# Rope's tables from TensorE, bias and norm rows spread by TensorE, and cosine products in place in PSUM

## The chip, the cores and the metric

The kernel runs on one core of a Trainium2 chip. Its time is the time on the device in microseconds (us), from the start of the program to its end. Engines are named as the profile names them: PE is TensorE (PEld its weight loads), DVE is VectorE, ACT is ScalarE, POOL is GpSimd, SP is the engine that here only issues DMAs. An entry such as SPq or ACTq is the sequencer of an engine, which issues DMAs.

## What is computed

A block of linear attention and a gated feed-forward layer (RWKV's channel mixing), each followed by a layer norm over the sum with its input. The input has 16 sequences of 1024 tokens with 512 channels in fp32. Only the attention half is touched by the change:

```python
qkv = x @ Wqkv.T + bqkv
q, k, v = split(qkv)
q = q * rsqrt(mean(q*q) + eps) * gq      # rmsnorm, the same for k with gk
k = k * rsqrt(mean(k*k) + eps) * gk
# rope, per head of 32 channels, position l: pairs (r, i)
out_r = r*cos[l] - i*sin[l];  out_i = r*sin[l] + i*cos[l]
qf, kf = relu(q), relu(k)
# per sequence and head: sum over l of [v, 1] x kf, applied to qf, divided by the last row
```

The launch puts the channels of q and k in an order in which each head has its 16 real parts first and then its 16 imaginary parts.

## The kernel before

**Tiles.** Work goes by tiles of 128 tokens: 128 tiles, 8 to a sequence (a block). Each tile of x is loaded twice, turned (`xt`, channels on partitions) for the projections and straight (`xn`) for the sum over tokens. Every fp32 operand of a product is split into two halves, `h` (a cast to fp32r) by ScalarE and `l` (the remainder) by VectorE, and a product is three passes (h by h, h by l, l by h). A projection of one tile to q or to k is therefore 4 chunks of channels by 3 passes, 12 products of 512 columns into one PSUM bank (`proj`, L415 to L429).

**One slot a tile.** `slot(i)` (L579) is called for i from 0 to 127. In it: the projections q(i) and k(i); the halves of the next tile's `xt` (`split_x`, L284) and of this tile's `xn`; `add_kx(i - 1)` (L465), 12 products that add k times x of the tile before into four banks `kx0` to `kx3` of a pool of their own; `rope(i)`; then `tables(i + 1)` and `seed(i + 1)`. Ends of blocks add `finish_a` to `finish_c`. From the sixth slot on one further weight chunk is loaded and split a slot (`late_weight`). The feed-forward half follows from 1200 us on; a few of its tiles are drawn into the slots.

**Seeds and banks.** Products that are not on the `kx` banks take banks from a ring of four (`mm`, `bank`, L97). Before a projection ScalarE copies the bias row, which lies spread over all partitions in `b_qk`, into its bank (`seed`, L318, by `seeded`, L136), and the products add to it. A bank can be seeded again once rope has read it for the last time.

**Rope.** `rope` (L433) reads q, then k, from PSUM: ScalarE takes the sum of squares (L438); VectorE multiplies by the sine table into `t2` (L441), by the cosine table into `ro` (L442), and adds the two with halves of heads swapped (L443). q goes to DRAM as `q_d`; k is scaled and cut at zero by ScalarE (L451), cast to `kh` (L454), and VectorE makes `kl` (L455). POOL makes the reciprocal root (L121) and the running sum of k over a block (L460, L462).

**Tables.** The tables hold the norm weight times cosine or sine for the 128 positions of a tile, one each for q and k: four of 128 by 512 (`tables`, L330). Since a sequence has 8 tiles, they are computed for tiles 0 to 7 and stored to DRAM (`tab_d`, L349); later tiles load them (L340). Each has a single buffer. POOL computes them with two forms of multiply (L345 for cosine, L348 for sine), from the norm weights spread over partitions (`g_qk`) and from `cos` and `sn`.

**The start (L352 to L386).** Eight products on zeros; the load of the first `xt`; `b_qk` and `g_qk` as loads that spread a row over 128 partitions (512 KB each); the eight weight chunks of q and k (n = 0 to 3 for q, 4 to 7 for k), loaded in turn by SP's and ScalarE's queues, each split by `split_w` (L310).

**Order.** The lists of each engine are not the order of the source: a planner simulates the program with its own costs and lays out each engine's instructions, taking what is ready and giving what comes first in the source the first claim. On the chip every engine then works through its list in order.

Of the kernel before, what the change touches and what calls it, by code (L numbers as in the profile page):

```python
# [8 lines left out]
F32 = mybir.dt.float32  # L9
# [25 lines left out]
def kernel(  # L35
# [41 lines left out]
    def f32(ap):  # L77
        return ap.bitcast(F32)
# [186 lines left out]
    with ExitStack() as a_ctx:  # L265
# [56 lines left out]
        def rows(tl):  # L322
            return tl.rearrange("p (h i) -> p h i", i=HH)

        def halves(tl):
            return tl.rearrange("p (h two i) -> p h two i", two=2, i=HH)
# [3 lines left out]
        def tables(i):  # L330

            t = i % 8
            if i < 8:
                tab_d[t] = dram.tile([P, 2, 2, DIM], F32, name=f"tab_d{t}")
            for j in range(2):
                for n in (1, 0):
                    tb = wa.tile([P, DIM], F32, tag=f"tab{j}{n}", name=f"tab{j}{n}{i}")
                    tab[i, j, n] = tb
                    if i >= 8:
                        nc.sync.dma_start(out=tb, in_=tab_d[t][:, j, n, :])  # L340
                        continue
                    g = g_qk[:, j * DIM : (j + 1) * DIM]
                    if n == 0:
                        c = cos[:, t, :].unsqueeze(1).to_broadcast([P, 2 * HEADS, HH])
                        G.tensor_mul(rows(tb), rows(g), c)  # L345
                    else:
                        c = sn[:, t, :, :].unsqueeze(1).to_broadcast([P, HEADS, 2, HH])
                        G.tensor_mul(halves(tb), halves(g), c)  # L348
                    nc.sync.dma_start(out=tab_d[t][:, j, n, :], in_=tb)  # L349


        m0 = te.tile([P, 2, DIM], F32R, tag="m", bufs=2, name="m0")  # L352
        V.memset(f32(m0[:, 0, :]), 0.0)
        for n in range(8):
            T.matmul(bank(f"pswarm{n}"), lhsT=m0[:, 0, 0:P], rhs=m0[:, 0, :], start=True, stop=True)
        load_xt(0)
        b_qk = ca.tile([P, 2 * DIM], F32, name="b_qk")
        nc.scalar.dma_start(out=b_qk, in_=bqkv[0 : 2 * DIM].partition_broadcast(P))
        split_x(0)
        g_qk = wp.tile([P, 2 * DIM], F32, tag="m", bufs=NC_, name="g_qk")  # L360
        cos = ca.tile([P, 8, HH], F32, name="cos")
        sin = tp.tile([P, 8, HH], F32, tag="y", bufs=2, name="sin")

        sn = ca.tile([P, 8, 2, HH], F32, name="sn")
        for j in range(2):
            cols = slice(j * DIM, (j + 1) * DIM)
            for c in range(NC_):
                n = NC_ * j + c
                split_w(
                    w_qk["h"][:, c, cols],  # L370
                    w_qk["l"][:, c, cols],
                    wqkv[:, c, cols],
                    V,
                    (nc.sync, nc.scalar)[c % 2],
                    *(("x", XA), ("q", 3))[n >= XA],
                )
            if j == 0:
                seed(0)
                nc.scalar.dma_start(out=g_qk, in_=gqk.partition_broadcast(P))
                nc.sync.dma_start(out=cos, in_=cos_t)  # L380
                nc.sync.dma_start(out=sin, in_=sin_t)
                G.tensor_copy(sn[:, :, 0, :], sin)
                G.tensor_scalar(sn[:, :, 1, :], sin, -1.0, None, ALU.mult)
                tables(0)
        load_xt(1)
        load_xn(0)  # L386
        mu, omm = {}, {}

        def constants():
# [43 lines left out]
        def rope(i, ps):  # L433
# [3 lines left out]
            for j in range(2):  # L437
                S.activation(junk(f"{i}{j}"), ps[j], AF.Square, accum_out=ss[:, j : j + 1])  # L438
                r = wa.tile([P, DIM], F32, tag=f"ro{j}", bufs=1 + j, name=f"ro{j}{i}")
                t2 = wa.tile([P, DIM], F32, tag="t2", name=f"t2{j}{i}")  # L440
                V.tensor_mul(t2, ps[j], tab.pop((i, j, 1)))  # L441
                V.tensor_mul(r, ps[j], tab.pop((i, j, 0)))  # L442
                V.tensor_add(halves(r), halves(r), halves(t2)[:, :, ::-1, :])  # L443
                ro.append(r)
                if j == 0:
                    q_d[i] = dram.tile([P, DIM], F32, name=f"q_d{i}")
                    nc.sync.dma_start(out=q_d[i], in_=r)
            V.tensor_scalar(ss, ss, 1.0 / DIM, RMS_EPS, ALU.mult, ALU.add)  # L448
            rsqrt(rstd_all[:, i, :], ss)
            k = ro[1]  # L450
            S.activation(k, k, AF.Relu, scale=rstd_all[:, i, 1:2])  # L451
            kh = tk.tile([P, DIM], F32R, tag="kh", bufs=2, name=f"kh{i}")
            kl = tk.tile([P, DIM], F32R, tag="kl", bufs=2, name=f"kl{i}")
            S.copy(kh, k)  # L454
            V.tensor_sub(kl, k, f32(kh))  # L455
            b, t = divmod(i, 8)
            ros[i] = k
# [111 lines left out]
        def late_weight():  # L569
# [6 lines left out]
            split_w(m[:, 0, :], m[:, 1, :], w[:, c, :], V, nc.sync)  # L576
            nc.sync.dma_start(out=w_d[n][:, c, :, :], in_=f32(m))

        def slot(i):  # L579
            last = i == N - 1  # L580
            if i + 2 < N:
# [1 line left out]
            b, t = divmod(i - 2, 8)  # L583
            if b >= 0 and t == 7:
                finish_a(b)
            qk = [proj(i, 0), proj(i, 1)]
            if not last:
                split_x(i + 1)
            split_xn(i)
            if not last:  # L590
# [9 lines left out]
            state[i] = rope(i, qk)  # L600
            if not last:
                tables(i + 1)
                seed(i + 1)
            if i == 2:
                with tc.issue_after(load.ins):
                    constants()
# [277 lines left out]
```

## Time and profile before

| what | value |
|---|---|
| median of 3 runs | 2749.24 us (2747.41 to 2749.43) |
| profiled execution, own time | 2751.16 us |
| profiled execution, span of the core | 2749.4 us |
| granted TensorE clock, mean | 0.996 |
| products (and transposes) issued | 12520 |
| PE busy, 0 to 8 us | 3.80 us |
| PE busy, 20 to 28 us | 8.00 us |
| PE busy, 1300 to 2749 us | 1441.93 of 1449 us |
| DMA, 0 to 8 and 8 to 20 us | 237 and 268 GB/s |

The profile is of one execution. Its span runs from the first to the last instruction of the core; the own time of that execution is 1.8 us more. PE's busy time counts overlapping products once, so that it says little about how close they follow each other; the number of products in a stretch, times the spacing of two that follow directly, says more. A group's line gives source line, engine, operation, output and inputs, shape and count, then busy time and the mean duration of one in ns, then how long the engine had stood idle before them and for whom. A line on waits names the waiting engine and line, whom it waited for, and the total, the number and the longest of the waits.

### The profile page before, as it was taken

What the parts mean: (1) busy time and instruction counts of PE and PEld (TensorE: products, weight loads), DVE (VectorE), ACT (ScalarE), POOL (GpSimd) and SP (SyncE); (2) the same over time, 40 slices, a digit from 0 to 9 for tenths busy, and PEclk for the clock granted to TensorE, in tenths of its full rate; (3) what the DMA queues carried; (4) which work ended last, traced back from release to release, by engine and by line L of the source; (5) the groups of instructions that cost most, each with busy time, mean ns of one, the idle gap of its engine ahead of it and who ended that gap; (6) DMA issues with size and microseconds to landing.
All of it is one profiled execution on the core that took longest, in us unless ns stands there. A gap on an engine that the chain in (4) does not pass through costs nothing.

```text
span 2749.4 us, 40113 instructions
## 1 busy us (share of the span) xinstructions
PE 2698.3 (98%) x12520; PEld 2227.0 (81%) x12520; DVE 2197.8 (80%) x4874; ACT 1878.3 (68%) x3807; POOL 724.5 (26%) x804
## 2 busy tenths in 40 slices
PE   8899999999999999998999999999999999999998
PEld 6687888888888788876888888888888888888887
DVE  8888887788888788878787878788787878787874
ACT  4566655666655556557777777777777777777775
POOL 6421222222222222223222222222222222222221
PEclk9999999999999999999999999999999999999999
DMA  6698778777777777764323231322223232313210
GB/s 216 217 308 292 235 234 265 226 229 222 222 227 230 228 236 241 236 216 163 102 65 108 93 115 55 114 89 91 86 92 108 66 108 92 116 54 116 69 58 31
DMA packets 230854, 431.17 MB, mean 157 GB/s; under 512 B 24544, under 2 KB 24800, under 8 KB 230640
## 3 DMA queue, kind: packets, MB, share of 16 engines
q1 hardware_dynamic: 229776, 426.51, 48.6%
q10 hardware_dynamic: 864, 2.10, 0.2%
q8 instruction: 99, 1.62, 0.2%
q14 instruction: 115, 0.94, 0.1%
HBM read 313.14 MB, written 115.38 MB: 156 GB/s over the span
## 4 chain that ended last, share of the span: by engine, by line
PE 66%; DVE 11%; issue 5%; DMA 5%; ACT 4%; POOL 1%; SPq 0%; DVEq 0%; ACTq 0%; POOLq 0%
PE psk L157 13%; PE psr L157 12%; PE psv L157 12%; PE psy L157 12%; PE pskx L477 4%; PE psq L421 4%; PE psk L421 3%; DVE ro L442 3%; DVE t L441 2%; PE pst L142 2%; PE psqt L142 2%; DMA q_d<-ro 2%; DVE ro L443 2%; DMA q<-q_d 1%; DVE kl L455 1%
## 5 line engine op out<-in xcount | busy, mean ns | idle before, releaser
L157 PE MATMUL psk<-mkh,w_k 128*128 128x512 f32 x1024 | 336.8, 396 | 0.0
L157 PE MATMUL psv<-w_v,kah 128*128 128x512 f32 x1024 | 321.8, 395 | 2.3 <-DVE qtl L213 1.2
L157 PE MATMUL psr<-w_r,mrh 128*128 128x512 f32 x1024 | 322.7, 396 | 1.1 <-ACT r L693 1.1
L157 PE MATMUL psy<-mb,qth 128*128 128x512 f32 x1024 | 316.7, 391 | 3.1 <-ACT qth L212 3.1
L121 POOL TENSOR_TENSOR rstd_all<-ss,mhalf 128x2 f32<-128x2 f32 x128 | 111.1, 868 | 682.7 <-DVE ss L448 651.9
L157 PEld LDWEIGHTS psy<-mb,qth 128*128 128x128 f32 x1024 | 192.5, 188 | 43.4 <-ACT qth L212 3.6
L249 DVE TENSOR_TENSOR y<-psy,g_out 128x512 f32<-128x512 f32 x128 | 88.3, 690 | 171.9 <-PE psy L157 171.6
L157 PEld LDWEIGHTS psk<-mkh,w_k 128*128 128x128 f32 x1024 | 192.3, 188 | 39.1
L157 PEld LDWEIGHTS psv<-w_v,kah 128*128 128x128 f32 x1024 | 187.6, 188 | 39.2 <-DVE qtl L213 1.6
L157 PEld LDWEIGHTS psr<-w_r,mrh 128*128 128x128 f32 x1024 | 187.5, 188 | 38.2 <-ACT r L693 1.5
L668 POOL TENSOR_TENSOR mkl<-mixk,mkh 128x512 fp32r<-128x512 f32 x128 | 175.6, 1372 | 144.0 <-ACT mkh L667 144.0
L421 PE MATMUL psq<-wqk_h,xh 128*128 128x512 f32 x512 | 202.3, 395 | 5.3 <-ACT wqk_h L313 2.7
L421 PE MATMUL psk<-wqk_h,xh 128*128 128x512 f32 x512 | 200.4, 391 | 1.4 <-ACT wqk_h L313 1.3
L421 PE MATMUL psk<-wqk_l,xh 128*128 128x512 f32 x512 | 200.1, 391 | 1.3 <-DVE wqk_l L314 1.3
L157 PE MATMUL psr<-w_r,mrl 128*128 128x512 f32 x512 | 200.7, 392 | 0.0
L157 PE MATMUL psy<-mb,qtl 128*128 128x512 f32 x512 | 200.4, 391 | 0.2 <-DVE qtl L213 0.2
L421 PE MATMUL psq<-wqk_h,xl 128*128 128x512 f32 x512 | 200.5, 392 | 0.0
L421 PE MATMUL psq<-wqk_l,xh 128*128 128x512 f32 x512 | 200.2, 391 | 0.2 <-DVE wqk_l L314 0.2
L157 PE MATMUL psv<-w_v,kal 128*128 128x512 f32 x512 | 200.1, 391 | 0.0
L421 PE MATMUL psk<-wqk_h,xl 128*128 128x512 f32 x512 | 199.8, 390 | 0.0
L157 PE MATMUL psk<-mkl,w_k 128*128 128x512 f32 x512 | 199.7, 390 | 0.0
L136 ACT COPY psk<-b_qk 128x512 f32<-128x512 f32 x128 | 75.8, 593 | 161.2 <-DVE ro L442 159.0
(147 smaller groups left out, 7219.1 us busy)
## 6 DMA issues: line engine op xcount, KB each, us to landing
tab<-tab_d SPq DMA_DIRECT2D x480, 256.0 KB
xt<-in_xt_dram SPq DMA_DIRECT2D x128, 256.0 KB
xn<-in_x_dram SPq DMA_DIRECT2D x128, 256.0 KB
q_d<-ro SPq DMA_DIRECT2D x128, 256.0 KB
m_d<-m SPq DMA_DIRECT2D x64, 512.0 KB
mb<-m_d SPq DMA_DIRECT2D x64, 512.0 KB
q<-q_d SPq DMA_DIRECT2D x128, 256.0 KB
x<-in_x_dram SPq DMA_DIRECT2D x128, 256.0 KB
```

What stands on the lines that cost most here:

```text
L121: G.tensor_tensor(dst, src, mhalf[:, 0 : src.shape[1]], ALU.pow)
L136: S.copy(ps, src)
L142: T.matmul(ps[:, n * P : (n + 1) * P], lhsT=b, rhs=ident, is_transpose=True, start=(n == 0), stop=(n == NC_ - 1), skip_group_check=True,)
L157: T.matmul(ps, lhsT=a[u][:, rows], rhs=b[w][:, cols], start=(afresh and c == 0 and k == 0), stop=(c == n - 1 and k == 2), skip_group_check ...
L249: V.tensor_mul(y, ps, g_out)
L421: T.matmul(ps, lhsT=a[i][:, c, :], rhs=w_qk[b][:, c, cols], start=False, stop=(c == NC_ - 1 and n == 2), skip_group_check=True,)
L441: V.tensor_mul(t2, ps[j], tab.pop((i, j, 1)))
L442: V.tensor_mul(r, ps[j], tab.pop((i, j, 0)))
L443: V.tensor_add(halves(r), halves(r), halves(t2)[:, :, ::-1, :])
L455: V.tensor_sub(kl, k, f32(kh))
L477: T.matmul(ps_kx[b][c], lhsT=a[:, c * P : (c + 1) * P], rhs=r, start=(t == 0 and n == 0), stop=(t == 7 and n == 2),)
L668: (V if n == "r" and s != 1 else G).tensor_sub(ml, m, f32(mh))
```

## The change

- `tables` for tiles 0 to 7: each table is one product on TensorE with 96 rows, `cs` (cosine and sine of the tile's positions, turned, in a high half twice and a low half) by `gt` (a mask that picks the angle's row, times the norm weight, in high and low halves). ScalarE copies the result to the table's buffer. Tiles 0 and 1 use the `kx` banks, the others the ring of four.
- The rows of bias and of norm weight are loaded as four rows of 2 KB into partitions 0, 32, 64 and 96 of a zeroed tile, split into halves, and spread over the partitions by products with 0/1 matrices (`sel_b`, `sel_g`). The bias goes straight into the banks of the first tile's q and k and is copied from there to `b_qk`.
- Five products on zeros in place of eight. The weights of q are split first, then the angles and norm weights are prepared, then the weights of k, with the load of the second `xt` behind the first of these. The second tile's seed and projection q(1) come ahead of k(0).
- `rope`: the cosine product is written in place in its PSUM bank, and the add reads it from there. `kh` is made by an activation of its own from k, ahead of the one that scales and cuts k.

```diff
@@ tables(i) @@
-                    g = g_qk[:, j * DIM : (j + 1) * DIM]
-                    if n == 0:
-                        c = cos[:, t, :].unsqueeze(1).to_broadcast([P, 2 * HEADS, HH])
-                        G.tensor_mul(rows(tb), rows(g), c)
-                    else:
-                        c = sn[:, t, :, :].unsqueeze(1).to_broadcast([P, HEADS, 2, HH])
-                        G.tensor_mul(halves(tb), halves(g), c)
+                    ps = kx_bank(2 * j + n) if i < 2 else bank(f"pstab{i}{j}{n}")
+                    T.matmul(ps, lhsT=cs[0:KT, t, :], rhs=gt[j][0:KT, n, :], start=True, stop=True)
+                    S.copy(tb, ps)
                     nc.sync.dma_start(out=tab_d[t][:, j, n, :], in_=tb)
+        def kx_bank(c):
+            return pa.tile([P, DIM], F32, tag=f"kx{c}", bufs=1, name=f"psb{c}")
@@ the start @@
-        for n in range(8):
+        for n in range(5):
             T.matmul(bank(f"pswarm{n}"), lhsT=m0[:, 0, 0:P], rhs=m0[:, 0, :], start=True, stop=True)
+        row = tp.tile([P, DIM], F32, tag="q", bufs=3, name="row")
+        V.memset(row, 0.0)
         load_xt(0)
+        for n, (src, j) in enumerate(((bqkv, 0), (bqkv, 1), (gqk, 0), (gqk, 1))):
+            nc.scalar.dma_start(
+                out=row[n * DH : n * DH + 1, :],
+                in_=src[j * DIM : (j + 1) * DIM].unsqueeze(0),
+            )
+        angle = [tp.tile([P, 8, HH], F32, tag="y", bufs=2, name=f"angle{n}") for n in range(2)]
+        for n, src in enumerate((cos_t, sin_t)):
+            nc.scalar.dma_start(out=angle[n], in_=src)
...
+        S.copy(row_h, row)
+        V.tensor_sub(row_l, row, f32(row_h))
         b_qk = ca.tile([P, 2 * DIM], F32, name="b_qk")
-        nc.scalar.dma_start(out=b_qk, in_=bqkv[0 : 2 * DIM].partition_broadcast(P))
+        for j in range(2):
+            first[0, j] = bank(f"ps{'qk'[j]}0")
+            for n, r in enumerate((row_h, row_l)):
+                T.matmul(first[0, j], lhsT=sel_b[:, j, :], rhs=r, start=(n == 0), stop=(n == 1))
+            S.copy(b_qk[:, j * DIM : (j + 1) * DIM], first[0, j])
         split_x(0)
...
+        for c in range(NC_):
+            split_qk(0, c)
+        cs3 = wp.tile([P, 8, P], F32, tag="m", bufs=NC_, name="cs3")[:, :, 0:KT]
+        for n in range(2):
+            G.tensor_copy(
+                cs3.rearrange("p t (r n i) -> p t r n i", r=3, n=2)[:, :, :, n, :],
+                angle[n].unsqueeze(2).to_broadcast([P, 8, 3, HH]),
+            )
...
+            for t in range(NC_):
+                T.matmul(ps[0:KT, t * P : (t + 1) * P], lhsT=cs3[:, NC_ * n + t, :], rhs=ident, is_transpose=True, ...)
+            S.copy(cs[0:KT, part, :], groups(ps)[0:KT])
+            low = slice(2 * DH, KT)
+            V.tensor_sub(cs[low, part, :], groups(ps)[low], f32(cs[low, part, :]))
...
+            for n, r in enumerate((row_h, row_l)):
+                T.matmul(ps, lhsT=sel_g[:, j, n, :], rhs=r, start=(n == 0), stop=(n == 1))
+            V.tensor_mul(halves(gt[j][:, 1, :]), halves(ps), msk[:, 1:3, :]...)
+            V.tensor_mul(rows(gt[j][:, 0, :]), rows(ps), msk[:, 0, :]...)
+        split_qk(1, 0)
         load_xt(1)
+        for c in range(1, NC_):
+            split_qk(1, c)
         load_xn(0)
+        seed(1)
+        tables(0)
@@ rope(i, ps) @@
-                V.tensor_mul(r, ps[j], tab.pop((i, j, 0)))
-                V.tensor_add(halves(r), halves(r), halves(t2)[:, :, ::-1, :])
+                V.tensor_mul(ps[j], ps[j], tab.pop((i, j, 0)))
+                V.tensor_add(halves(r), halves(ps[j]), halves(t2)[:, :, ::-1, :])
...
-            S.activation(k, k, AF.Relu, scale=rstd_all[:, i, 1:2])
-            S.copy(kh, k)
+            S.activation(kh, k, AF.Relu, scale=rstd_all[:, i, 1:2])
+            S.activation(k, k, AF.Relu, scale=rstd_all[:, i, 1:2])
@@ slot(i) @@
-            qk = [proj(i, 0), proj(i, 1)]
-            if not last:
+            if i == 0:
+                qk = [proj(0, 0)]
+                split_x(1)
+                ahead.append(proj(1, 0))
+                qk.append(proj(0, 1))
+            else:
+                qk = [ahead.pop() if ahead else proj(i, 0), proj(i, 1)]
+            if 0 < i < N - 1:
                 split_x(i + 1)
```

## The prediction

> **What bounds the kernel now.** I read the page's first part, then busy time by stretches, then TensorE's waits in the stretch that loses most, then the groups of that stretch. The page:
>
> ```profile
> PE 2698.3 (98%) x12520; PEld 2227.0 (81%) x12520; DVE 2197.8 (80%) x4874; ACT 1878.3 (68%) x3807; POOL 724.5 (26%) x804
> ```
>
> TensorE sets the time. At full clock a 512-column product follows the one before after 0.227 us (starts 22.29, 22.52, 22.74 in the timeline), so a product added costs 0.227 us and the only other thing to win is time in which none is issued. Where that lies (stretch: length, busy time and count of each engine):
>
> ```profile
> core 0: us, PE busy (x) PEld busy (x) DVE busy (x) ACT busy (x) POOL busy (x), PEclk, DMA share, GB/s
> 8.00:20.00 12.00, 9.23 (x24) 6.46 (x25) 8.95 (x9) 6.69 (x13) 7.20 (x6) 0.72 0.76 268
> 28.00:125.00 97.00, 83.85 (x349) 63.78 (x348) 84.79 (x112) 50.94 (x107) 57.66 (x42) 0.98 0.63 211
> 125.00:300.00 175.00, 173.06 (x792) 141.74 (x792) 146.06 (x252) 108.63 (x229) 38.20 (x36) 1.00 0.85 281
> 300.00:1200.00 900.00, 892.18 (x4103) 741.42 (x4102) 728.35 (x1271) 536.38 (x1143) 202.56 (x190) 1.00 0.74 233
> 1200.00:1300.00 100.00, 86.23 (x406) 68.42 (x405) 78.16 (x174) 65.81 (x131) 34.63 (x35) 0.98 0.53 179
> ```
>
> From 28 to 125 us there are 349 products: 333 of 512 columns, 8 of 256 and 8 of 128, at 0.227, 0.171 and 0.108 us: 77.8 us of work in 97, so 19.2 us are lost. In 300 to 1200 the same count of start-to-start excess gives 4.6 us. Who is waited for, 28 to 125 (total, times, longest):
>
> ```profile
> PE pskx L477 <- ACT kh L454: 8.7, 8, 2.4
> PE pskx L477 <- DVE kl L455: 3.3, 4, 1.0
> PE pskv L520 <- DVE ro L442: 0.7, 1, 0.7
> PE psq L421 <- ACT psq L136: 0.3, 1, 0.3
> ```
>
> These are 13.0 us; the rest is the slow restart after each wait and half clock at 50 to 53 us. kh and kl come late because rope does. The groups of 28 to 125, and the add again in 300 to 1200 (last line):
>
> ```profile
> L345 POOL TENSOR_TENSOR tab<-g_qk,cos 128x512 f32<-128x512 f32 x13 | 22.0, 1691 | 0.0
> L348 POOL TENSOR_TENSOR tab<-g_qk,sn 128x512 f32<-128x512 f32 x12 | 16.8, 1403 | 9.4 <-DVE t L441 9.3
> L443 DVE TENSOR_TENSOR ro<-ro,t 128x512 f32<-128x512 f32 x20 | 19.4, 972 | 0.2
> L442 DVE TENSOR_TENSOR ro<-psq,tab 128x512 f32<-128x512 f32 x10 | 6.8, 681 | 1.3 <-DMA q_d<-ro 1.3
> ...
> L443 DVE TENSOR_TENSOR ro<-ro,t 128x512 f32<-128x512 f32 x194 | 133.2, 687 | 2.7
> ```
>
> While POOL multiplies tables, VectorE's operations with both inputs in SBUF grow (the add 972 against 687 ns, xnl 1286 against 895, kl 1192 against 772); those with one input in PSUM do not (681).
>
> **Part 1, tables on TensorE.** POOL loses 38.8 us in that stretch. VectorE gets back 20 x 0.285 + 10 x 0.39 + 10 x 0.42 + 9 x 0.44 (L448, 599 against 158 ns) = 17.8 us, and stands at 67 us instead of 85. ScalarE gets four copies a tile at 0.59 us (its copies and squares read or write PSUM in 0.59): 28 of them for tiles 1 to 7, 16.5 us, on top of 50.9: 76% of some 89 us. TensorE gets 28 products, +6.4 us, on the path. The 19.2 us: at 300 to 1200 the loss is under 0.1 us a tile with VectorE at 81%, but here ScalarE is fuller, four PSUM banks serve six tiles a turn (q, k, four tables), and a table's copy must wait until rope has read the table before it (one buffer each), with the seeds queued behind it on ScalarE. Chain from the end of q: square 0.78, t2 0.69, copy 0.59, seed 0.59, some 0.5 of handovers: 3.2 us, against k (2.7) and kx (2.7) as cover. Bounds 1 and 12 us of loss; I take 0.5 us a tile, 4.0: **-15.2 and +6.4**.
>
> **Part 2, the start.** Two 512 KB broadcasts go; 5.1 MB land in the first 20 us, 255 GB/s, so k's weights, whose casts waited until 13.0 and 14.9 us, can land 3 to 4 us sooner. Against it: row loads wait for a memset and their six small issues (four rows, two angles, 0.35 us each) stand on ScalarE's queue with two of q's four weights. A landing also holds up unrelated issues:
>
> ```profile
> SPq L381 <- DMA b_qk<-in_bqkv_dram: 3.0, 1, 3.0
> ```
>
> The load of sin waited for the bias to land; more transfers ahead of the weights make more such turns, the small ones short. First product of q before: 7.98 us. After: rows landed about 5.2 (issue at 2 to 3; xt took 4.9 us beside a broadcast, so 4.5 to 7.9 are the ends, and 2 KB rows are taken near the lower), row_h 0.62, row_l 0.69, two products 0.5, copy of the bank to b_qk 0.59 before q may accumulate in it, handovers 0.4: 8.0. VectorE's list to the end of xl(1): row_l, xl(0), 8 weight halves and xl(1), 11 x 0.62; 2 low angles, 4 gt (one PSUM input each), 6 x 0.62; masks 0.5; POOL's copy of the angles (0.76 us for 128 elements, so 2.3 for each 384) slows it, as the tables did, by some 2: 13 us from 5.9, so 19. q(1) then takes 2.7: q(0), k(0), q(1) done at 22.2; before, q(0) and k(0) at 20.2 and 12 more products at 22.9. The 8 transposes, 8 bias and norm products and 4 of tables(0) fit in TensorE's idle time meanwhile (2.7 us ahead of 7.98, 2.8 from 8 to 20). **-0.7**, bounds -4 (the transfers decide) and +4 (VectorE and the queues decide; without that idle cover the added 16 to 20 products would cost some 3.5 themselves).
>
> The warm-up drops from eight to five. The timeline shows q's products 0.43 us apart from 9.0 to 12.0 although eight ran before, so nothing is lost. [...] I take 0.
>
> **Part 3, in place in PSUM.** No row has VectorE writing PSUM; nearest are 681 ns for reading it and ScalarE's 590 either way: I take 0.68. The add now reads PSUM. [...] The add no longer grows beside POOL (one input in PSUM), and the product no longer waits for the store of q (18.0 us of VectorE idle in 300 to 1200); the add does, later. What costs: the bank is free at the add's end, not at the product's: 0.72 us later at least, 1.3 at the median, since the planner puts another operation between. Seed by seed in 300 to 1200, the time between seed end and first product has a lower tenth of 0.64, a quartile of 1.47 and a median of 2.9 us. Pushing those that waited for L442 by 0.72 us and changing nothing else costs 3.6 us, by 1.3 us 11.4; pushing all 193, 6.6 and 24.6. The planner lays the order anew with the later release in it; bounds 0 and 20, I take **+1.5**.
>
> **Part 4, the rest.** kh comes from one activation (0.72) instead of two (0.72 + 0.62), 0.6 us sooner a tile; ScalarE pays 0.1, hidden at 60% busy. q(1) ahead of k(0) moves xt(1) ahead of three weights on SP, counted above. Tables' stores stay, 32 of them on SP, now behind ScalarE's copies; xt and xn loads queue behind those, earlier than before because the tables are. The handover at 1200 to 1300 loses 18.8 us and is ordered anew: 0, give or take 3.
>
> **Sum.** -15.2 + 6.4 - 0.7 + 1.5 = -8.0. The profiled execution took 2751.2 us (span 2749.4); it becomes 2743.2. It lies 1.9 above the median of the runs, so the median goes from 2749.24 to **2741.2**.
>
> **Rivals.** (a) *Better*: the transfers decide the start (-4), stalls nearly vanish (-2 more), -14: 2735. For it: casts at 13 to 15 us wait for DMA. Against: VectorE's list. (b) *ScalarE and the banks take POOL's place* in tiles 1 to 7: 12 us stay lost, 0 in all: 2749. For it: ScalarE already stands 22.6 us before psk's seed. Against: those waits were for L442 on a slowed VectorE. (c) *Banks held longer*, on the other side: if the planner's order does not absorb the later release through some 120 tiles, seeds come late every second tile: 11.4 to 20 us in place of 1.5, 2757. It decides once it costs 9.5 us, which is 1.2 us of extra hold for those that waited. Against: psq waits only 2.1 us for its seed in 900. (d) *The tables' time was hidden anyway* is excluded by the 8.7 us on kh.
>
> **How the numbers follow.** Forecast 0.48, own range 2736 to 2746; (a) 0.17; (b) 0.15; (c) 0.20. A change under 0.2% (5.5 us) is about what this kernel's measurement cannot tell from none. Faster (under 2743.7): 0.37 + 0.17 + 0.02 = 0.56; within: 0.11 + 0.10 + 0.04 = 0.25; slower (over 2754.7): 0.03 + 0.16 = 0.19. Range 2732 to 2756: below it a twentieth, above it most of (c).
>
> **What would show it.** Right: POOL under 25% busy from 28 to 125 us, the add at 0.69 there, TensorE's waits for kh and kl under 4 us, 36 products done by 22 us. Wrong: psq or psk waiting for L136, or tables waiting for a bank, for more than 5 us; a first product of q after 10 us; start-to-start excess of more than 10 us in 300 to 1200.

## The result, and the profile after

The changed kernel takes **2739.0 us** (median of 5 runs, 2738.3 to 2743.0) against 2749.4 (5 runs beside it, 2747.4 to 2750.9): a ratio of **0.9962, 95% interval 0.9948 to 0.9976**, or 10.4 us less. The forecast was 2741.2, 8.0 less. The profiled execution of the changed kernel took 2738.3 (span 2736.4) and was the quickest of its five; that of the kernel before, at 2751.2, was slower than all five beside it. So the two traces lie 13.0 us apart, and a sum made from them is to be held against 13.0.

The page of the changed kernel, its first part:

```profile
PE 2701.2 (99%) x12565; PEld 2240.0 (82%) x12565; DVE 2157.3 (79%) x4895; ACT 1909.0 (70%) x3842; POOL 678.9 (25%) x772
```

TensorE issues 45 products more and still ends sooner. Busy time of three stretches, with the columns of the table in the prediction:

```profile
8.00:20.00 12.00, 8.59 (x23) 6.47 (x22) 9.38 (x15) 8.40 (x16) 0.00 (x0) 0.72 0.47 163
28.00:125.00 97.00, 93.43 (x406) 74.77 (x405) 69.46 (x122) 68.05 (x142) 22.61 (x19) 0.98 0.68 226
300.00:1200.00 900.00, 897.14 (x4139) 746.92 (x4138) 725.70 (x1280) 545.55 (x1148) 208.55 (x191) 1.00 0.73 234
```

From 28 to 125 us TensorE issues 406 products where it issued 349; POOL falls from 57.7 to 22.6 us busy, VectorE from 84.8 to 69.5, ScalarE rises from 50.9 to 68.1. The row that the forecast did not see coming is 300 to 1200: 897.1 us busy for 892.2, and 36 products more in the same 900 us. The row of 8 to 20 shows no gain at all.

Who TensorE waits for from 28 to 125 us (total, times, longest), where kh and kl had cost 12.0 (the lines for kh and for the tables; kl is not among them any more):

```profile
PE pskx L553 <- ACT kh L529: 1.7, 1, 1.7
PE pstab L343 <- ACT tab L344: 0.5, 1, 0.5
PE pstab L343 <- DVE ro L519: 0.4, 1, 0.4
```

And the groups of that stretch which answer to the costs in the prediction:

```profile
L344 ACT COPY tab<-pstab 128x512 f32<-128x512 f32 x24 | 13.5, 588 | 4.2 <-PE psk L497 1.7 <-DMA tab_d<-tab 0.9 <-issue 0.8
L343 PE MATMUL pstab<-gt,cs 96*128 96x512 f32 x24 | 8.6, 428 | 1.0 <-ACT tab L344 0.5 <-DVE ro L519 0.4
L518 DVE TENSOR_TENSOR psk<-psk,tab 128x512 f32<-128x512 f32 x11 | 7.6, 688 | 0.0
L519 DVE TENSOR_TENSOR ro<-psq,t 128x512 f32<-128x512 f32 x10 | 6.9, 688 | 1.4 <-DMA q_d<-ro 1.3
```

The add is back from 972 to 688 ns, the product written to PSUM in place takes 688, the table's copy 588. Tables wait for a bank or a buffer for 0.9 us in all.

**Where the time went.** For each stretch I summed, over TensorE's products in order, the time from one start to the next less the product's own spacing (0.227, 0.171 or 0.108 us for 512, 256 or 128 columns: the usual steps behind L421, L520 and the transposes of L142 in the kernel before). Together with the products added (32 of tables, 8 of bias and norm, 8 transposes, 3 zero products fewer: 9.3 us, of which 6.4 lie after 28 us) it accounts for the two spans:

| stretch, us | excess before | excess after | products added | change | forecast |
|---|---|---|---|---|---|
| 0 to 28 (start) | 11.5 | 11.2 | +2.9 | +2.6 | -0.7 |
| 28 to 125 (tiles 1 to 7) | 19.5 | 7.3 | +6.4 | -5.8 | -8.8 |
| 125 to 300 | 2.5 | 2.2 | 0 | -0.3 | 0 |
| 300 to 1200 | 4.6 | -3.5 | 0 | -8.1 | +1.5 |
| 1200 to the end | 26.8 | 25.3 | 0 | -1.5 | 0 |
| sum | 64.9 | 42.5 | 9.3 | -13.1 | -8.0 |

(A sum below nothing comes above all from kv's products of 128 columns: the next one starts some 0.06 us after them, not 0.108, at 185 of 192 of them from 300 to 1200 us before (L528, -8.7 us) and 188 of 192 after (L604, -9.1 us). Only differences are used.) Two terms are wrong by 3 us or more against the change, one by 10 us for it.

### The profile page after: what moved, and what is told of

It reads as the page before. It is cut to its first block, busy times and chain, and to the rows that moved or that the text cites. A ratio compares the mean times of both kernels' runs of the same rounds, so it can differ in the third digit from the quotient of the medians.

```text
span 2736.4 us, 40284 instructions
## 1 busy us (share of the span) xinstructions
PE 2701.2 (99%) x12565; PEld 2240.0 (82%) x12565; DVE 2157.3 (79%) x4895; ACT 1909.0 (70%) x3842; POOL 678.9 (25%) x772
## 4 chain that ended last, share of the span: by engine, by line
PE 86%; DVE 4%; issue 1%; DMA 1%; ACT 1%; POOL 0%; POOLq 0%; DVEq 0%; ACTq 0%; SPq 0%
PE psk L157 13%; PE psr L157 13%; PE psy L157 12%; PE psv L157 12%; PE psq L497 10%; PE pskx L553 10%; PE psk L497 10%; PE pst L142 2%; PE psqt L142 2%; PE psm L633 1%; PE pskv L596 1%; DMA q<-q_d 0%; DVE ro L519 0%; PE pskv L604 0%; DMA tab<-tab_d 0%
## 5 line engine op out<-in xcount | busy, mean ns | idle before, releaser
L538 POOL TENSOR_TENSOR acc<-acc,ro 128x512 f32<-128x512 f32 x96 | 156.1, 1626 | 294.3 <-ACT ro L530 203.8
L121 POOL TENSOR_TENSOR rstd_all<-ss,mhalf 128x2 f32<-128x2 f32 x128 | 92.8, 725 | 545.0 <-DVE ss L524 492.4
L121 POOL TENSOR_TENSOR yrs<-yss,mhalf 128x1 f32<-128x1 f32 x128 | 71.2, 556 | 466.8 <-DVE yss L252 319.2
```

Of the source, the lines that this page charges most:

```text
L121: G.tensor_tensor(dst, src, mhalf[:, 0 : src.shape[1]], ALU.pow)
L538: G.tensor_add(acc[b], acc[b], k)
```

## The experiments

All are timed over five rounds beside the kernel before. An edit is made on the kernel before or on the changed one, as each says; "of 2749.4" below is one less the ratio, times 2749.4 us. A trace is of one execution, and executions of one kernel differ (those of e2 lie between 2740.6 and 2753.1 us), so a few microseconds between two traces need not come from the kernels.

| kernel | median, us | ratio, 95% interval | of 2749.4 |
|---|---|---|---|
| changed | 2739.0 | 0.9962, 0.9948 to 0.9976 | -10.4 |
| e2 start and tables alone | 2747.2 | 0.9985, 0.9973 to 0.9996 | -4.1 |
| e6 kh alone | 2746.7 | 0.9986, 0.9977 to 0.9994 | -3.8 |
| e5 in place alone | 2730.1 | 0.9923, 0.9911 to 0.9935 | -21.2 |
| e3 in place and kh | 2737.5 | 0.9952, 0.9939 to 0.9965 | -13.2 |
| e1 start, tables and kh | 2740.5 | 0.9964, 0.9950 to 0.9977 | -9.9 |
| e9 start, tables and in place | 2734.3 | 0.9941, 0.9928 to 0.9955 | -16.2 |
| e4 changed, eight zero products | 2735.5 | 0.9941, 0.9927 to 0.9955 | -16.2 |
| e7 before, tables loaded | 2744.8 | 0.9980, 0.9970 to 0.9989 | -5.5 |
| e8 changed, tables loaded | 2736.0 | 0.9942, 0.9930 to 0.9954 | -15.9 |
| e10 changed, b_qk from its own banks | 2735.0 | 0.9946, 0.9934 to 0.9958 | -14.8 |
| e11 changed, k(0) ahead of q(1) | 2741.1 | 0.9967, 0.9954 to 0.9980 | -9.1 |
| e12 e10 without the kh edit | 2731.9 | 0.9935, 0.9920 to 0.9950 | -17.9 |

### e2: start and tables alone

The changed kernel with both edits of rope undone: the cosine product goes to SBUF again, and k's activation and its copy to kh stand as before.

```diff
-                V.tensor_mul(ps[j], ps[j], tab.pop((i, j, 0)))
-                V.tensor_add(halves(r), halves(ps[j]), halves(t2)[:, :, ::-1, :])
+                V.tensor_mul(r, ps[j], tab.pop((i, j, 0)))
+                V.tensor_add(halves(r), halves(r), halves(t2)[:, :, ::-1, :])
...
+            S.activation(k, k, AF.Relu, scale=rstd_all[:, i, 1:2])
...
-            S.activation(kh, k, AF.Relu, scale=rstd_all[:, i, 1:2])
-            S.activation(k, k, AF.Relu, scale=rstd_all[:, i, 1:2])
+            S.copy(kh, k)
```

> The changed kernel with both edits of rope undone (cosine product in SBUF, kh cast from the scaled k), so the start and the tables alone. If the two halves of the change add up as the traces place them (about -3 us until 300 us, about -9 behind): 2746 to 2748. If the edits of rope do nothing and the tables or the order did it all: 2738 to 2741.

Measured 2747.2: the part that the change is mostly made of brings 4.1 us. Its excess from 28 to 125 us is 7.6, as in the changed kernel (7.3); so the early tiles are mended by the tables alone. But from 300 to 1200 it is 5.6 and not -3.5. The steady gain is not the tables'.

### e1: the cosine product to SBUF again

The changed kernel with only the first two lines of the diff above undone.

> The changed kernel with the cosine product written to SBUF again, all else as changed. [...] Theory C (the prediction's: the longer hold of the bank costs): 2736 to 2738.

Measured 2740.5, an interval that lies on that of the changed kernel: on top of the tables and the kh edit, in place is worth nothing that can be told. The steady excess stays low (-2.8 for -3.5), so there the kh edit does by itself what in place does.

### e3: rope's edits alone

On the kernel before: both edits of rope, nothing of the start or the tables.

```diff
-                V.tensor_mul(r, ps[j], tab.pop((i, j, 0)))
-                V.tensor_add(halves(r), halves(r), halves(t2)[:, :, ::-1, :])
+                V.tensor_mul(ps[j], ps[j], tab.pop((i, j, 0)))
+                V.tensor_add(halves(r), halves(ps[j]), halves(t2)[:, :, ::-1, :])
...
-            S.activation(k, k, AF.Relu, scale=rstd_all[:, i, 1:2])
...
-            S.copy(kh, k)
+            S.activation(kh, k, AF.Relu, scale=rstd_all[:, i, 1:2])
+            S.activation(k, k, AF.Relu, scale=rstd_all[:, i, 1:2])
```

> The kernel before with only the two edits of rope. If these give the steady part's gain: 2740 to 2743, with 4 to 5 us of TensorE waits less in 300 to 1200. If the prediction's sign holds (bank held longer): 2750 to 2752. If their gain is only in the stretch in which POOL makes tables (the add no longer grows beside POOL): 2744 to 2747, and 300 to 1200 as before.

Measured 2737.5, as fast as the whole change. With POOL making the tables as before, four lines of rope give the whole gain. Its excess is 14.9 from 28 to 125 us and -4.8 from 300 to 1200.

### e5 and e6: the two edits of rope, one at a time

On the kernel before: e5 has the first two lines of e3's edit, e6 the rest.

> The kernel before with the cosine product in place in PSUM and nothing else. Theory A (the gain behind 300 us comes from kh, in place gives little): 2747 to 2751, and from 600 to 1200 us TensorE's excess stays at 2 us or more. Theory B (it comes from the add and the store's wait): 2740 to 2743. The prediction's term (the bank held longer) is +1.5 here: 2751.

> The kernel before with kh made by its own activation ahead of k's, and nothing else. Theory A: 2739 to 2743, kh ready 2 to 3 us sooner after k's last product, the shortest slack of kl before its product (a twentieth of 0.06 us before) over 1 us. Theory B: 2747 to 2750.

In place alone takes **2730.1**, 21.2 us off, the best of all kernels run, and its interval (0.9911 to 0.9935) lies clear of the changed kernel's (0.9948 to 0.9976). The kh edit alone takes 3.8 us off. The trace of e5 puts its gain at 7.6 us from 28 to 125 (19.5 to 11.9), 10.0 from 300 to 1200 (4.6 to -5.4) and 5.9 after 1200 (26.8 to 20.9). e6 has the steady gain too, 7.9 us (4.6 to -3.3), and lacks the first (20.4).

The change had been feared for the banks that it holds, so the seeds (L136) come first here. Of the waits of all engines from 300 to 1200 us, these lines are on the seeds and on the store of q; the kernel before:

```profile
ACT psk L136 <- DVE ro L442: 114.5, 66, 4.2
ACT psq L136 <- DVE ro L442: 63.8, 46, 2.9
DVE ro L442 <- DMA q_d<-ro: 18.0, 12, 2.1
```

The same lines of e5, in place alone, where VectorE has no wait for the store left:

```profile
ACT psk L136 <- DVE ro L443: 64.9, 37, 2.9
ACT psq L136 <- DVE ro L443: 23.8, 18, 3.9
```

And of e6, the kh edit alone:

```profile
ACT psk L136 <- DVE ro L442: 118.1, 68, 5.1
ACT psq L136 <- DVE ro L442: 49.1, 43, 3.4
DVE ro L442 <- DMA q_d<-ro: 3.6, 4, 1.5
```

In place halves the time for which ScalarE stands ahead of the seeds (178 to 89 us; some 24 go over to waits for another operation of VectorE). But e6 has the same steady gain with 167 us of that wait, so the seeds are not what the steady gain comes from. What TensorE itself waits for, in the same stretch, says more. Before:

```profile
PE pskv L520 <- DVE kv L538: 4.2, 4, 2.5
PE psq L421 <- ACT psq L136: 2.1, 4, 0.7
PE pskx L477 <- DVE kl L455: 1.1, 2, 0.7
```

Of the changed kernel:

```profile
PE pskv L596 <- DVE ro L519: 1.4, 2, 0.7
PE pskx L553 <- DVE kl L531: 1.1, 2, 0.6
PE pskx L553 <- ACT kh L529: 0.4, 1, 0.4
```

The waits of 4.2 us for kv and of 2.1 us for q's seeds are gone; all three sit behind rope on VectorE's list. The largest, for kv (at a block's end VectorE reads it from one half of a bank before TensorE's products go on in the other), can be followed in the trace of the kernel before:

```profile
492.81 0.69 DVE L442 TENSOR_TENSOR ro<-psq,tab 128x512 f32<-128x512 f32 x1 [1.17 <-DMA q_d<-ro]
493.41 0.34 DVE L538 SCALAR_TENSOR_TENSOR kv<-ksv,bv,pskv 128x128 f32<-128x128 f32 x1
493.81 0.58 PE L520 MATMUL pskv<-kx,wa_h 128*128 128x256 f32 x1 [2.49 <-DVE kv L538]
```

kv stands on VectorE's list right behind the cosine product of q, and this product waits until the q before it is stored, since its buffer `ro` is the only one for q. The other three waits for kv have the same form, with 0.91 to 1.37 us on the store. Behind the longest, the clock granted to TensorE (third number from the end) was 0.61 from 494 to 498 us, where it had been 1.00 from 480 to 490, and the products that followed lost a further 1.5 us by their spacing:

```profile
494.00:498.00 4.00, 4.00 (x16) 3.54 (x17) 4.00 (x9) 0.94 (x3) 1.08 (x1) 0.61 0.79 225
```

In all three kernels with neither edit of rope (before, e2, e7) VectorE waits 17.3 to 18.3 us for the store of q and TensorE 4.2 to 4.5 us for kv; in the eleven with one or both it is at most 7.0 and 0.5. To see which chain has more room, I measured four times in nine kernels. *Hold* is from a projection's last product to the operation that frees its bank (lower tenth and median); *seed room* is from a seed's end to its first product (lower tenth); *k chain* is from k's last product to the end of kh (median); *kl room* is from the end of kl to the product that reads it (lower twentieth). Hold and seed room are over 300 to 1200 us, the others over 600 to 1200.

| kernel | in place | kh | hold | seed room | k chain | kl room | excess, 300 to 1200 |
|---|---|---|---|---|---|---|---|
| before | no | no | 3.54, 5.04 | 0.65 | 8.22 | 0.06 | 4.6 |
| e2 | no | no | 3.33, 4.92 | 1.06 | 8.18 | 0.06 | 5.6 |
| e7 | no | no | 3.18, 4.87 | 0.76 | 8.16 | 0.06 | 10.5 |
| e6 | no | yes | 2.10, 3.42 | 1.42 | 5.95 | 0.79 | -3.3 |
| e1 | no | yes | 2.11, 3.66 | 1.71 | 6.22 | 1.10 | -2.8 |
| e5 | yes | no | 2.90, 4.82 | 1.16 | 7.39 | 1.17 | -5.4 |
| e9 | yes | no | 2.90, 4.70 | 1.27 | 7.20 | 1.69 | -7.1 |
| e3 | yes | yes | 2.80, 4.46 | 1.61 | 5.38 | 1.35 | -4.8 |
| changed | yes | yes | 2.79, 4.43 | 1.35 | 5.34 | 1.48 | -3.5 |

The rooms sort the kernels: with neither edit, a kl ends just as its product starts and a seed comes early by 1.1 us or less, and these three kernels alone have an excess above nothing in the steady part. Either edit of rope gives kl a further 0.7 to 1.6 us and lowers the excess by 7.9 to 12.7 us, and both together find little more to take. **The steady gain is a rope that ends sooner, and each edit earns it by itself.** Most of the loss came through kv: 4.2 us of waiting and the 1.5 of spacing behind the longest, of 8.1 (1.4 us of waits of the same products, for rope's add, are left in the changed kernel). The seeds and kl have 3.2 us of waits before. That kl has more room does not explain the gain by itself: taken from 300 us on, its lower twentieth is only 0.2 us in e6 and in the changed kernel, and e12 (in place, no kh), which is not in the table, has 0.1 from 600 us on and an excess of -4.7. In place takes away the product's wait for the store of q, as its edit says; why the kh edit alone cuts that wait from 18.0 to 3.6 us is not shown.

The hold that had been feared is there, in its pure form: among kernels with kh, in place lengthens the lower tenth by 0.7 us (2.10 to 2.80) and the median by 0.8 to 1.0. Against the kernel before it is shorter all the same, since rope's operations come sooner, and seed room is wider in all four kernels with it (1.16 to 1.61 for 0.65). It costs nothing that shows.

### e9: the changed kernel without the kh edit

```diff
+            S.activation(k, k, AF.Relu, scale=rstd_all[:, i, 1:2])
...
-            S.activation(kh, k, AF.Relu, scale=rstd_all[:, i, 1:2])
-            S.activation(k, k, AF.Relu, scale=rstd_all[:, i, 1:2])
+            S.copy(kh, k)
```

> The changed kernel with kh cast from the scaled k as before, so start, tables and the product in place. If kh's edit spoils part of what in place gives (alone 2730, with kh 2737): 2731 to 2735. If it is only that the start costs what it brings and the two edits of rope reach for the same loss: 2738 to 2741.

Measured 2734.3, faster than with the edit by 5.8 us by the ratios, though the two intervals overlap. With e1 to e6 this completes all eight combinations of three parts: start and tables, in place, kh. They do not add. In place is worth 21.2 us alone, 12.1 on the start and tables, 9.4 on kh and 0.5 on both. The kh edit is worth 3.8 alone and 5.8 on the start and tables, and costs 8.0 on in place and 5.8 on in place with the start and tables. For both steps of 5.8 and for the 0.5 the intervals of the two kernels overlap; for the others they are clear of each other.

Part of that is read above: each edit of rope earns the same steady loss. And part may have a place, though no cause: on the start and tables, the stretch 1200 to 1300 us, where the second half of the kernel takes over, has an excess of 14.2 to 14.9 us in the three kernels without the kh edit (e2, e9, e12) and of 17.6 to 21.5 in the six with it (the changed one, e1, e4, e8, e10, e11). From e9 to the changed kernel it is 5.1 us (14.5 to 19.6). But these two traces end only 1.0 us apart: from 125 to 300 us alone e9 has 4.4 us more excess, so they cannot place the 5.8.

### e7 and e8: tables of tiles 1 to 7 loaded, not made

e7 is the kernel before, e8 the changed one; in both the tables of tiles 1 to 7 are loaded from the place where tile 0's were stored, so neither POOL (e7) nor TensorE and ScalarE (e8) make them. The work of 28 tables and their 28 stores is left out, and 28 loads take their place; rope then works with the wrong positions.

```diff
-            if i < 8:
+            if i == 0:
...
-                    if i >= 8:
-                        nc.sync.dma_start(out=tb, in_=tab_d[t][:, j, n, :])
+                    if i >= 1:
+                        nc.sync.dma_start(out=tb, in_=tab_d[0][:, j, n, :])
```

> The kernel before, with the tables of tiles 1 to 7 left out: those tiles and all later ones load tile 0's from DRAM, as many transfers as the stores were (so rope is computed with the wrong positions). No engine pays for tables then. If POOL's multiplies made the 19 us that TensorE loses from 28 to 125 us: 15 us or more of it go, 2733 to 2735. If the late kh lies in the order of the chain and POOL only adds to it: 5 to 9 us go, 2740 to 2744.

> The changed kernel with the same left out: the 28 products and copies of tiles 1 to 7 are gone and the tables loaded. The products' price by count is 6.4 us, and what the copies and banks add is small by the waits (1.0 us on pstab): 2731 to 2733. If the products lie in time that TensorE would have waited anyway: 2736 to 2739.

e7 asks whether POOL's multiplies were what made kh late. Its busy time from 28 to 125 us, and the add and kl in the groups of that stretch:

```profile
28.00:125.00 97.00, 88.62 (x389) 71.60 (x388) 71.92 (x124) 55.32 (x117) 21.19 (x19) 0.98 0.73 230
```

```profile
L443 DVE TENSOR_TENSOR ro<-ro,t 128x512 f32<-128x512 f32 x20 | 13.8, 689 | 0.2
L455 DVE TENSOR_TENSOR kl<-ro,kh 128x512 fp32r<-128x512 f32 x11 | 7.5, 683 | 0.0
```

POOL is down to 21.2 us, VectorE to 71.9, the add to 689 ns and kl from 1192 to 683: the slowing is POOL's doing, shown. But the waits of TensorE in the stretch stay:

```profile
PE pskx L477 <- ACT kh L454: 8.4, 6, 3.4
```

The excess falls from 19.5 to 11.2 only (and the kernel gains still less, 5.5 us, since its excess from 300 to 1200 us is 10.5 for 4.6). So POOL explains 8 of the 19 us; the kh wait, 8.7 before and 8.4 here, is not VectorE's slowness. In e2, where TensorE makes the tables and rope is as before, that wait is gone too (0.4 us). What differs is that e2's stretch is ordered anew around 28 more products, which stand between k and kx as cover. That reading fits the counts, and e8 bears it out in part. There the 28 products are left out of the changed kernel, and kx waits 4.9 us for kl and kh from 28 to 125 us, against 1.7 with them:

```profile
PE pskx L553 <- DVE kl L531: 3.3, 3, 1.6
PE pskx L553 <- ACT kh L529: 1.6, 1, 1.6
```

Only in part, because e8's order is laid anew as well.

e8 prices the 28 products: without them the changed kernel is 5.5 us faster by the ratios (the intervals overlap) and 2.3 by the spans (2734.1 for 2736.4), with 2.4 us more excess in the stretch (9.7 for 7.3). Some of their 6.4 us were filling waits.

### e10 and e12: b_qk from banks of its own

e10 lays TensorE's copy of the bias rows a second time into two other banks, four products more, and fills b_qk from these; q's and k's first banks are then free of that copy. e12 is e10 with the kh edit undone as in e9.

```diff
-            S.copy(b_qk[:, j * DIM : (j + 1) * DIM], first[0, j])
...
+        for j in range(2):
+            ps = kx_bank(j)
+            for n, r in enumerate((row_h, row_l)):
+                T.matmul(ps, lhsT=sel_b[:, j, :], rhs=r, start=(n == 0), stop=(n == 1))
+            S.copy(b_qk[:, j * DIM : (j + 1) * DIM], ps)
```

> The changed kernel with b_qk made by four further products in banks of their own, so that q of the first tile needn't wait until its bank was copied (TensorE waits 3.4 us there). Theory (that copy, queued behind four weight casts on ScalarE, is what puts the first product of q at 13.5 us): the first product at 9 to 10 us, the first three projections done 2 to 3 us sooner, 2736 to 2738. Rival (the halves of the weights set the time anyway): the first product sooner, the 36th not, 2738 to 2740.

> Start and tables with b_qk from banks of its own, the product in place, kh as before: the edits that helped so far together. If the tables on TensorE are worth their products once the start no longer waits: 2725 to 2729, under the 2730 of the product in place alone. If they only exchange POOL's stalls for products and copies: 2729 to 2733.

The question is why the changed kernel's first product of q starts at 13.5 us and not at 8.0. TensorE's longest wait in its first 28 us:

```profile
PE psq L497 <- ACT b_qk L389: 3.4, 1, 3.4
```

And the timeline of the changed kernel, ScalarE's list ahead of that copy and the product behind it (start, duration, operation, idle time before it):

```profile
8.66 0.62 ACT L313 CAST wqk_h<-wstage 128x512 fp32r<-128x512 f32 x1 [1.87 <-DMA wstage<-in_wqkv_dram]
...
10.14 1.14 ACT L313 CAST wqk_h<-wstage 128x512 fp32r<-128x512 f32 x2
11.17 0.62 ACT L287 CAST xh<-xt 128x512 fp32r<-128x512 f32 x1
11.69 0.62 ACT L302 CAST xnh<-xn 128x512 fp32r<-128x512 f32 x1
12.36 0.62 ACT L313 CAST wqk_h<-wstage 128x512 fp32r<-128x512 f32 x1
12.88 0.58 ACT L389 COPY b_qk<-psq 128x512 f32<-128x512 f32 x1
...
13.51 0.80 PE L497 MATMUL psq<-wqk_h,xh 128*128 128x512 f32 x1 [3.41 <-ACT b_qk L389]
```

The copy L389 takes 0.58 us, but it stands on ScalarE's list behind four weight casts, the first of which waits 1.87 us for its load, two casts of the angles (in the lines left out) and those of x and xn; q may not accumulate in the bank until it is read. In e10 the first product of q starts at 11.8 and the 36th of the projections ends at 21.5 us instead of 25.7. Its busy time from 8 to 20 us:

```profile
8.00:20.00 12.00, 11.82 (x43) 9.60 (x44) 10.53 (x17) 9.05 (x19) 0.00 (x0) 1.00 0.51 167
```

43 products for 23, four of them the added ones. Of the 4.2 us, 1.7 are the earlier first product. The rest is spacing: in e10 no wait parts the bias products from q's, and from 12.9 us on the products are 0.227 us apart; in the changed kernel those behind the wait of 3.41 us are 0.43 apart until 19.2.

The lead does not last. Counted in products issued, each at its spacing and the added four left out, e10 is 3.2 us ahead at 26 us and 0.7 at 32, because TensorE then waits for a bank for the tables, behind rope's add (0 to 40 us):

```profile
PE pstab L343 <- DVE ro L523: 2.8, 2, 2.1
```

It is 2.7 ahead again at 125 us, and the two traces end 1.7 apart. The time is 2735.0, 4.4 us less than the changed kernel by the ratios, with overlapping intervals. So e10 shows what holds up the first product; how much of the 4.4 us comes from there is not shown. e12 at 2731.9 takes this and drops kh; it does not beat e5.

### e4: eight zero products

```diff
-        for n in range(5):
+        for n in range(8):
```

> The changed kernel with eight products on zeros instead of five. Theory (the clock is half until about 4 us of real work whatever stands ahead): within 1 us of the changed kernel, 2738 to 2740; q's first ten products still 0.43 us apart. Rival (five are too few to bring the clock up): 2 us faster, 2737. What it differs by besides shows how far a mere new plan moves the time.

TensorE's timeline at the start of e4:

```profile
6.83 0.50 PE L388 MATMUL psq<-row_h,sel_b 128*128 128x512 f32 x1 [0.24 <-ACT row_h L382]
7.16 0.39 PE L388 MATMUL psk<-row_h,sel_b 128*128 128x512 f32 x1
7.39 0.62 PE L444 MATMUL psb<-row_h,sel_g 128*128 128x512 f32 x2
7.86 0.40 PE L388 MATMUL psq<-row_l,sel_b 128*128 128x512 f32 x1
...
11.52 0.50 PE L497 MATMUL psq<-wqk_h,xh 128*128 128x512 f32 x1 [2.58 <-ACT b_qk L389]
```

And of the changed kernel, with five:

```profile
6.97 0.78 PE L388 MATMUL psq<-row_h,sel_b 128*128 128x512 f32 x1
7.54 0.63 PE L388 MATMUL psk<-row_h,sel_b 128*128 128x512 f32 x1
7.97 1.05 PE L444 MATMUL psb<-row_h,sel_g 128*128 128x512 f32 x2
8.82 0.58 PE L388 MATMUL psq<-row_l,sel_b 128*128 128x512 f32 x1
9.24 0.40 PE L388 MATMUL psk<-row_l,sel_b 128*128 128x512 f32 x1
9.47 0.63 PE L444 MATMUL psb<-row_l,sel_g 128*128 128x512 f32 x2
```

With eight, the bias products are 0.23 us apart at once (7.16, 7.39, and 7.86 after two), with five 0.43 (7.54, 7.97) until 9.24, and 0.23 from there. Both then wait for b_qk, and both lose the quick spacing by it: with five, after 3.41 us, q's products are 0.43 apart from the start until 19.2; in e4, after 2.58 us, the first four are still quick (11.52, 11.85, 12.09, 12.32), then spacing is 0.43 or more from 12.7 to 19. So the theory fits the kernel before (q's first product at 7.98 us, 0.43 apart until 12.0) and not e4. The 36th projection product ends 0.8 us sooner than in the changed kernel (24.9 for 25.7).

The time fell by 5.8 us by the ratios (3.5 by the medians), with overlapping intervals. The start shows 0.8 of it, and the rest has no place in the traces, which end only 0.8 apart: -0.6 from 28 to 125, +1.3 to 300, -1.7 to 1200, +0.3 after. Three zero products in the first 7 us do no work for those stretches; what they can alter is the order that the planner lays. Order and the spread of executions are not told apart here, so I take **4 to 6 us as what the two can do together**, and no difference of that size between two of these kernels is put down to a cause without a place in the trace.

### e11: k(0) ahead of q(1)

```diff
-                qk = [proj(0, 0)]
+                qk = [proj(0, 0), proj(0, 1)]
                 split_x(1)
-                ahead.append(proj(1, 0))
-                qk.append(proj(0, 1))
```

> The changed kernel with k of the first tile ahead of the second tile's q again. If q(1) covers the wait for k's weights: the first 36 products end 1 to 3 us later, 2740 to 2742. If the planner takes what is ready and the order in the source weighs little: within 2 us of 2739.

2741.1, 1.3 us slower by the ratios with intervals that lie on one another, and the 36th product ends at 24.6 instead of 25.7. Putting q(1) ahead neither gains nor costs anything that shows.

## Why the prediction was right

The number was right and lies well within its range, by terms that were not. By the traces, the start was off by 3.3 us and tiles 1 to 7 by 3.0, both against the change, and 300 to 1200 us by 9.6 for it; that they offset each other is luck.

- **Tiles 1 to 7: right in kind, mis-sized.** POOL was busy 23% of the stretch (under 25% named), the add took 688 ns (0.69), the waits for kh and kl were 1.7 us (under 4). The excess fell by 12.2 us, not 15.2. The 28 products were priced at 6.4 us; leaving them out is worth 2.3 by the spans, 5.5 by the ratios. And the cause given, "kh and kl come late because rope does", with VectorE slowed by POOL as the reason, carries only 8 of the 19 us (e7). Rival (d), that the tables' time was hidden anyway, was excluded by the 8.7 us on kh; that wait stays without POOL's tables (8.4), and what excludes (d) are the 8 us that go.
- **The start: the failed step is "copy of the bank to b_qk 0.59".** The duration was right; its place on ScalarE's list was not looked at. The first product of q was to start at 8.0 and started at 13.5, the sign that the prediction itself named for being wrong (after 10 us). The second part of that step fell with it: the added products of the start, 2.9 us, were to fit "in TensorE's idle time meanwhile", but the excess of the start stayed at 11.2 us for 11.5 and they came on top. The sum is +2.6 where -0.7 was forecast, still within the +4 bound. e10 removes the wait and ends the projections 4.2 us sooner, most of which is lost again by 32 us. "36 products done by 22 us" was wrong as well (25.7); besides, the 19 and 2.7 us of that sum make 21.7, not the 22.2 that it used.
- **Fewer zero products: 0 was forecast, 0.8 us show at the 36th product (e4).** The bias products, which stand ahead of q, are 0.23 us apart with eight and 0.43 until 9.24 us with five. Little of this reaches q, because the wait for b_qk stands between (2.58 us with eight, 3.41 with five): most of q's products are 0.43 apart with five and with eight. "So nothing is lost" took the 0.43 of the kernel before for a fact about eight products; there, 2.7 us of idle time followed them.
- **In place: the failed step is the one that "costs" it, "the bank is free at the add's end, not at the product's".** The fact is right (0.7 us at the lower tenth where the kh edit is there on both sides), its duration too (688 ns for 0.68), and the add takes the same with one input in PSUM (688 ns) as with both in SBUF (687). But it was the only thing counted. The 18.0 us of VectorE idle for the store of q was named and given no worth, though four of its twelve waits held up kv and with it TensorE (4.2 us, and 1.5 of spacing), and what an earlier rope does was not asked outside tiles 1 to 7, since the steady loss was read as a small remainder. Forecast +1.5, measured -8.1 from 300 to 1200 in the whole change and -10.0 in e5. Rival (c) fell with the step: no kernel of the table with in place has an excess over -3.5 us in the steady part, for 4.6 before.
- **kh: counted at nothing, which it isn't.** "0.6 us sooner a tile" became 2.3 (8.22 to 5.95), since kh no longer stands behind k's own activation and what the planner puts between the two. Alone it is worth 3.8 us (1.6 to 6.3); in the whole change no gain from it shows (e9).
- Rival (a) was wrong on both counts: 7.3 us of the loss in tiles 1 to 7 are left, and the start does not gain. Rival (b) is out: tables waited 0.9 us for a bank or a buffer.

**What stays open.** That the parts don't add is explained in the steady part and in tiles 1 to 7, where several parts earn the same loss (e5 took 7.6 us there without the tables). Why kh on top of in place *costs* (8.0 us, e3 against e5) is not. Nor why all three together fall short of in place alone by 10.8 us by the ratios: against e5, the changed kernel's span is 8.5 us longer, +1.6 at the end of the projections, +1.8 from 28 to 125 (6.4 of products less 4.6 of excess), -1.4 to 300, +1.9 to 1200 and +4.4 after. No one stretch holds it, and after 1200 us the kernels differ in their order alone. The excess after 1300 us takes one of two values in all kernels, 5.6 to 5.8 or 7.9 to 8.0, and I didn't find what sets it; it lies evenly over that half, about 0.4 or 0.55 us in every 100. e4 says that some of this may be no more than the order. Why e2 lost the kh wait of tiles 1 to 7 and e7 did not is shown in part only (e8).

The version to use is **e5**: two lines of rope on the kernel before, 2730.1 us, ratio 0.9923 (0.9911 to 0.9935), 8.9 us under the changed kernel.

## What to carry to other kernels

An edit that holds a resource longer may still gain by what it no longer waits for: count both, and follow a small loss to what is waited for (here kv, behind a product that waits for the store of q) before calling it a remainder. A short copy on the path costs what stands ahead of it on its engine's list, not its own length (here 0.58 us, and TensorE waited 3.41). Run each part of a change alone where a planner orders the work: here two lines were worth more than the whole, two edits earned the same microseconds, and an edit without work in the measured stretches came out 3.5 us faster by the medians, about what kh alone is worth.

## What the runs showed of the hardware

- VectorE took 688 ns to write a 128x512 product into the PSUM bank that it reads (changed kernel, L518, 28 to 125 us), against 681 for the same product to SBUF (before, L442); the add took 688 with one input in PSUM (changed, L519) against 687 with both in SBUF (before, L443, 300 to 1200 us).
- Beside POOL's multiplies of the tables, VectorE's operations on SBUF took longer: with 36 us of POOL's time gone from 28 to 125 us (57.7 before, 21.2 in e7), the add went from 972 to 689 ns and kl from 1192 to 683. With one input in PSUM the add takes 684 to 687 ns in e5, where POOL is busy for 55.0 us of the same stretch.
- TensorE's quick spacing was lost again behind some waits (in brackets the start of the product that waited): in the changed kernel after 3.41 us (13.5) and in the kernel before after 2.49 us (493.8) at once; in e4 after 2.58 us (11.5), 1.1 us into the work that followed; in the kernel before after 2.41 us (49.2), 0.8 us into it; in the changed kernel after 2.00 us (182.8), 0.7 us into it. In the kernel before it was kept after waits of 1.78 us (94.1) and 2.88 us (1263.5). So the length of the wait alone does not tell these cases apart.
- The granted clock of the profile shows such a loss (0.50 from 13.0 to 19.2 us in the changed kernel, at 0.43 us a product), but not the slow spacing at the start: in the changed kernel it reads 1.00 from 7.0 to 9.3 us, where the bias products are 0.43 apart until 9.24, and in e10 1.00 from 8 to 20 us, though the products up to 12.6 us are 0.43 apart. There only the spacing of starts shows it.
